# A two-layer graph attention kernel: 22 chunks of rows straight from x, tiles turned two ahead, row buffers in a pool of their own

## The chip, the cores and the metric

The kernel runs on one core of a Trainium2 chip. Its time is the device time of one execution in microseconds (us), from the start of the program to its end, with all loads from and stores to device memory. Three runs of the kernel before gave 4555.35, 4556.34 and 4557.77 us.

## The reference

The graph has N = 6250 nodes with D = 256 features and E = 200000 edges, sorted by destination, with 32 attributes each. Cut to what matters:

```python
h = relu(layernorm(x))                               # rows are normalised over their 256 features
for l, H in ((0, 4), (1, 1)):                        # two layers of graph attention, 4 heads and 1
    te = relu(ea @ We + be) * exp(h @ Wo + bo)[src]  # features of the edges, gated by the source node
    s, d, e = edges and one self loop for each node  # a loop's e is the mean of the edges into its node
    hx = h @ Wg
    al = leaky_relu((hx @ a_s)[s] + (hx @ a_d)[d] + (e @ Wge) @ a_e, 0.2)
    al = softmax of al over the edges with one destination
    out = segment_sum(hx[s] * al, d) + bg + h        # relu of this after layer 0
    h = out
return x + (out + relu(layernorm(x)))
```

So each layer first needs a table with a row for each node (hx, two products with the attention vectors, and the gate), and then fetches 200000 rows of this table, one for each edge.

## The kernel before, in words

**Chunks, steps and tables.** Edges lie in order of destination, 128 to a chunk, one on each partition: 1563 chunks (NCH). 24 chunks make a step (C); a layer has 66 steps (NS), the last two shorter (14 and 13 chunks). The table of layer 0, T[0], has rows of 270 floats: hx, the attention products, the gate, and the two layer norm numbers of the node. Each step handles a window of at most 112 destination nodes.

**The prologue (L203 to L401)** makes T[0] and does all that is needed before the first step. The 6250 rows of x are 49 tiles of 128 rows (NT). They are loaded in groups: two tiles, then five, then seven each, of which the last seven are split into five and two. Four things happen to a tile.

- Its layer norm numbers come from `stats` of its group (L258): for each tile a bn_stats and a bn_aggr, on DVE (VectorE), then a reciprocal square root by three Newton steps (L273 to L298). For groups 0 to 2 these run on DVE; from group 3 on, POOL (GpSimd) does them, 15 instructions; for groups of rows that come straight from x (below) it is DVE again.
- `norm` (L309, ACT, which is ScalarE) makes h; `turn` transposes it with two matmuls into PSUM (L315, PE) and copies it to SBUF (L317, ACT); `mult` multiplies it with the weights (L430, PE); `keep` adds the bias and writes the table row to SBUF (L434, DVE).
- `store` (L332 to L334) finishes the rows of a group, two small ACT instructions, and sends one DMA on SP's queue to T[0].
- The loop at L356 sets the order by hand. In one pass k of it, tile k+3 is normalised, tile k+1 turned, tile k multiplied, and tile k−1 kept. Between these, `step` issues one instruction of the statistics of a later group, at most two groups ahead, and twice as often from the x rows on.

Step 0 does not use the table. Its 24 chunks (CX) are rows of x, fetched by source index with 24 indirect DMAs on POOL (`first_rows`, L247): eight before the loop, one in each pass from k = 4. They are tiles 49 to 72, in four groups of six, and go through the same pipeline into the buffer G0 of step 0. Nothing of them has to be stored. In between stands the index work (`indices` L436, one of its instructions in every second pass; `index_group` L561): numbers that say where segments begin and end, as penalties, flags and offsets. `indices` also writes a small table `flags` (L498) by DMA on SP. Penalties are written once for each of four heads, the copies on ACT (L602).

**The steps (L615 on).** For each step k the loop issues the gathers of the next step and the computation of this one. `gather` (L792) fetches 24 rows per partition from the table with 24 indirect DMAs on POOL (L799), each followed by a memset of a buffer that nobody reads (L803). Three buffers of gathered rows are used in turn, so the gathers of step k+3 go to the buffer of step k. `nodes` (L860) loads the rows of the destination window into one of five tiles (`tws`, cleared at L631). `spread` (L914), `rphase1`, `rphase2`, `adst` and `edge_rows` work out the part of the logits that comes from the edges; `logits` scans them with the penalties for maxima within segments; `scale` multiplies the gathered rows by their weights (L1095, DVE); `sums` adds up by destination with 24 matmuls (L1105); `evict` copies the sums out of PSUM (L1110, ACT), and from then on the buffer of the gathered rows is free. `finish` and `rows1` to `rows3` make the rows of the next layer's table, or of the output.

**What sets the order.** All code of prologue and steps stands under a manual schedule: each engine runs its instructions in the order in which the program issues them, and waits by semaphores for the buffers that it needs. Pools hand out SBUF; a buffer in a pool that opens later can lie where one of a closed pool was, and its first writer then waits for the last readers there. The gather buffers 1 and 2, `S` and the work tiles of the steps come after the prologue's pools.

Memory for gathered rows is `[128, 24, 270]` floats for each of three buffers. At the end `rows3` writes the output; its last rows go by an indirect DMA on POOL (L1249), and `flag` (L789) sums what `indices` found about the indices.

Of the kernel before, what the change touches and what calls it, by code (L numbers as in the profile page):

```python
# [22 lines left out]
F32 = mybir.dt.float32  # L23
# [11 lines left out]
NX = 24  # L35
# [44 lines left out]
class Kernel:  # L80
# [122 lines left out]
    def prologue(self):  # L203
# [7 lines left out]
        with ExitStack() as c:  # L211
            xp = self.pool("x", 1, c)
            wp = self.pool("pw", 2, c)
            pt = self.pool("pt", 2, c, space=PSUM)
            starts = sorted({*range(0, NT, GT), min(2, NT), max(NT - 2, 0)} - {NT})
# [11 lines left out]
            src0 = wp.tile([P, CX], I32, name="src0", bufs=1)  # L227
# [5 lines left out]
            warm = pt.tile([P, 2, P], F32, name="pT")  # L233
            for i in range(28):
                nc.tensor.matmul(warm[:, i % 2, :], self.ident, self.ident, start=True, stop=True)
            self.index_tiles()
            self.fixed_rows()
            zero = wp.tile([P, 2 * L.TW], F32, name="zero", bufs=1)
# [3 lines left out]
            trows = [wp.tile([P, GT, L.TW], F32, name=f"trow{i}", bufs=1) for i in range(3)]  # L242
# [12 lines left out]
            for _ in range(8):  # L255
                next(rows0, None)

# [43 lines left out]
            for i in range(0, CX, 6):  # L301
                xs[len(groups)] = G0[:, i:min(i + 6, CX), 0:D]
                groups.append(list(range(NT + i, NT + min(i + 6, CX))))
# [7 lines left out]
            def turn(g, i, t):  # L311
                pT = pt.tile([P, 2, P], F32, name="pT")
# [3 lines left out]
                hTs[t] = wp.tile([P, 2, P], F32, name="hT", bufs=3)  # L316
# [21 lines left out]
            for _ in range(6):  # L338
                next(lead, None)
            weave(lead, first)  # L340
            ahead = {g: stats(g) for g in range(1, len(groups))}

            def step(g):

                for q in list(ahead):
                    if q > g:
                        return
# [8 lines left out]
            for k in range(-3, len(tiles) + 1):  # L356
# [10 lines left out]
                if 0 <= k + 1 < len(tiles):  # L367
                    turn(*tiles[k + 1])
                if 0 <= k + 3 < len(tiles):
                    g, i, t = tiles[k + 3]  # L370
# [5 lines left out]
                if t >= NT:  # L376
                    step(g + 2)
# [3 lines left out]
                if t >= NT:  # L381
                    step(g + 2)
                if k >= 4:
                    next(rows0, None)
# [18 lines left out]
    def fixed_rows(self):  # L403
# [19 lines left out]
        for i in range(2):  # L423
            self.trow1.append(cp.tile([P, 2 * L1.TW], F32, name=f"t1row{i}"))
            nc.gpsimd.memset(self.trow1[i][:, L1.TW + D:], 0.0)

# [9 lines left out]
    def indices(self, wp):  # L436
# [4 lines left out]
        V = nc.vector  # L441
# [13 lines left out]
        V.tensor_copy(scf, sc0)  # L455
        V.memset(scf[:, 0, 0:1], 0.0)
        self.base_f = base = cp.tile([P, NS], F32, name="base")
        V.tensor_copy(base, scf[:, 0, :])
# [4 lines left out]
        V.tensor_sub(qd, base.unsqueeze(1).to_broadcast([P, 4, NS]), qbase)  # L463
# [1003 lines left out]
```

## Time and profile before

| quantity | value |
|---|---|
| median of three runs | 4556.34 us |
| profiled execution | 4555.93 us |
| its span in the profile | 4554.1 us |
| instructions | 37613 |
| PE, matmuls | 3065.9 us busy (67%), 9916 instructions |
| DVE | 2901.8 us (64%), 6675 |
| ACT | 516.8 us (11%), 1150 |
| POOL | 3915.8 us (86%), 6365 |
| granted TensorE clock, mean | 0.743 |
| read from device memory | 542.72 MB |

The profile is of one execution. A row of its groups names a line of the kernel, the engine, the operation and what it writes and reads, then how often, the busy time and the mean duration in ns; behind the second bar stands how long the engine was idle just before, and what released it. A row of the timeline gives the start of an instruction from the start of the span in us, how long it took, and in square brackets how long the engine had waited before it and for which instruction. "SPq" are the DMAs that SyncE issued, and an instruction that is released by "issue" waited for nothing that the trace shows. A row of the waits gives engine, line and releaser, then the time waited in all, how often, and the longest.

The slices of the span, each a fortieth of it or 114 us, tell the two parts apart: in the first one POOL is busy six tenths and ACT five; in all others up to the last POOL is at eight and ACT at one or none.

```profile
ACT  5111111111111111111100000000000000000000
POOL 6888888888888888888878888888888888888885
```

### The profile page before, as it was taken

Reading aid. Unit: us, or ns where it says so; the run is one execution under the profiler, and the core shown is the slowest. Engines: PE = TensorE matmul, PEld = TensorE weight load, DVE = VectorE, ACT = ScalarE, POOL = GpSimd, SP = SyncE. Lnnn points to the kernel's source line nnn. Section 1 sums busy time; section 2 is a strip of 40 time slices with the busy share of each in tenths; the row PEclk is TensorE's granted clock in tenths of the full one; section 3 lists DMA queues with packets and bytes.
Section 4 is the critical chain, followed back from the end, with each engine's and each line's share of the span. In section 5 each row is a group of like instructions: output and inputs, shape, how many; then the busy total and the mean of one; then the engine's idle time right before and its main releaser. Section 6 shows DMA issues by size and latency. Waiting matters only on the chain. (4 is left out here: it accounts for less than half of the span.)

```text
span 4554.1 us, 37613 instructions
## 1 busy us (share of the span) xinstructions
PE 3065.9 (67%) x9916; PEld 1899.5 (42%) x9916; DVE 2901.8 (64%) x6675; ACT 516.8 (11%) x1150; POOL 3915.8 (86%) x6365
## 2 busy tenths in 40 slices
PE   8777677667677677677746566666666665666665
PEld 6444444444444344444424334333343343433433
DVE  7877667677677677676745555555554555555655
ACT  5111111111111111111100000000000000000000
POOL 6888888888888888888878888888888888888885
PEclk9877777777777777777767777777777777777777
DMA  6444444444444444444434444444444444444442
GB/s 224 130 136 134 126 129 136 124 127 136 125 128 135 125 128 135 125 130 134 119 98 124 116 128 122 118 128 128 111 128 121 124 123 128 122 116 122 128 116 74
DMA packets 231112, 576.39 MB, mean 127 GB/s; under 512 B 63097, under 2 KB 87871, under 8 KB 230825
## 3 DMA queue, kind: packets, MB, share of 16 engines
q0 software_dynamic: 150144, 422.75, 35.2%
q1 hardware_dynamic: 80331, 150.52, 10.0%
q8 instruction: 79, 1.29, 0.1%
q14 instruction: 142, 1.16, 0.1%
q10 hardware_dynamic: 416, 0.67, 0.1%
HBM read 542.72 MB, written 31.09 MB: 126 GB/s over the span
## 5 line engine op out<-in xcount | busy, mean ns | idle before, releaser
L799 POOL DMA_INDIRECT G<-T,src x3102 | 2969.6, 957 | 553.1 <-issue 518.7
L1105 PE MATMUL u<-G,S 128*128 128x270 f32 (+1 forms) x6252 | 1461.0, 393 | 106.7 <-DVE G L1085 97.6
L1105 PEld LDWEIGHTS u<-G,S 128*128 128x128 f32 x6252 | 1189.5, 192 | 388.0 <-DVE G L1085 162.1
L803 POOL MEMSET gap<- 128x208 f32 x3102 | 893.3, 288 | 1.8
L1095 DVE TENSOR_TENSOR G<-G,kps 128x6144 f32<-128x6144 f32 (+3 forms) x136 | 853.0, 6274 | 0.0
L885 PE MATMUL y<-ea,webd 64*128 64x384 f32 (+1 forms) x1056 | 749.7, 860 | 67.3 <-ACT R L890 66.7
L1010 PE MATMUL lf<-ident,fb 128*36 128x128 f32 (+1 forms) x132 | 53.3, 404 | 1093.3 <-DVE fb L1002 772.3
L987 DVE TENSOR_TENSOR G<-rt,G 128x96 f32<-128x96 f32 (+1 forms) x132 | 30.2, 228 | 1138.9 <-DMA G<-T,src 1138.6
L1010 PEld LDWEIGHTS lf<-ident,fb 128*36 128x36 f32 (+1 forms) x132 | 15.7, 119 | 1134.6 <-DVE fb L1002 819.2
L899 PE MATMUL zad<-R,wea 128*64 128x384 f32 (+1 forms) x1056 | 476.0, 815 | 0.5 <-DVE aq L952 0.3
L890 ACT ACTIVATE R<-y,webd 128x768 f32<-128x768 f32 x260 | 233.2, 897 | 2015.2 <-PE lf L1027 1647.7
L930 DVE TENSOR_TENSOR S<-kps,loc 128x3072 f32<-128x3072 f32 x132 | 437.5, 3315 | 4.5
L885 PEld LDWEIGHTS y<-ea,webd 64*128 64x128 f32 x1056 | 300.9, 314 | 311.8 <-issue 192.5
L899 PEld LDWEIGHTS zad<-R,wea 128*64 128x64 f32 x1056 | 160.7, 207 | 319.0 <-issue 214.0
L945 PE MATMUL zad<-a,Q 128*128 128x12 bf16 (+1 forms) x132 | 24.9, 188 | 174.6 <-DVE a L943 174.6
L430 PE MATMUL fin<-wg,h1T 128*128 128x260 f32 x264 | 135.3, 667 | 2.3 <-ACT h1T L1200 2.3
L973 DVE STREAM_TRANSPOSE rt<-zad 128x768 f32<-128x768 f32 (+1 forms) x130 | 124.9, 960 | 12.1 <-PE zad L959 11.2
L914 DVE TENSOR_TENSOR lb<-lb,kps 128x1536 bf16<-128x1536 bf16 (+1 forms) x68 | 112.7, 1658 | 0.0
L1110 ACT ACTIVATE U<-u 128x270 f32<-128x270 f32 (+1 forms) x132 | 51.9, 393 | 493.7 <-PE u L1105 493.7
L1041 DVE SCALAR_TENSOR_TENSOR m<-fpen,lf,m 128x24 f32<-128x24 bf16 (+1 forms) x66 | 16.4, 249 | 132.8 <-PE lf L1027 132.6
L945 PEld LDWEIGHTS <-Q 128*128 128x128 bf16 x132 | 13.7, 104 | 208.3 <-DVE a L943 198.6
L430 PEld LDWEIGHTS fin<-wg,h1T 128*128 128x128 f32 x264 | 75.6, 316 | 52.1 <-issue 36.6
(201 smaller groups left out, 2287.5 us busy)
## 6 DMA issues: line engine op xcount, KB each, us to landing
G<-T,src POOLq DMA_INDIRECT x3102, 2.8
ea<-in_ea_dram SPq DMA_DIRECT2D x64, 768.0 KB
lb<-locrow SPq DMA_DIRECT2D x64, 384.0 KB
T<-t1row SPq DMA_DIRECT2D x66, 227.5 KB
tw<-T SPq DMA_DIRECT2D x66, 225.8 KB
tw<-T SPq DMA_DIRECT2D x66, 117.2 KB
tw<-in_x_dram SPq DMA_DIRECT2D x66, 112.0 KB
out_dram<-fb SPq DMA_DIRECT2D x64, 112.0 KB
```

The source lines that it names most:

```text
L430: self.nc.tensor.matmul(ps[:, :L.MW], hT[:, k, :], self.wg[L.l][:, k, :], start=(k == 0), stop=(k == 1))
L799: nc.gpsimd.indirect_dma_start(out=G[:, c, 0:L.TW], out_offset=None, in_=self.rows[L.l][0:n * (1 + L.l), :], in_offset=bass.IndirectOffset ...
L803: nc.gpsimd.memset(self.gap, 0.0)
L885: nc.tensor.matmul(y[:, o], self.webd[l][r, :], ea[r, w], start=True, stop=True)
L890: nc.scalar.activation(R[:, i, :32 * c].rearrange("p (b n) -> p b n", b=2), y.rearrange("p (b n) -> p b n", b=2)[:, :, :16 * c], AF.Relu, ...
L899: nc.tensor.matmul(st["zad"][i * PH:(i + 1) * PH, o], self.wea[l][0], R[:, i, w], start=True, stop=False)
L914: V.tensor_tensor(lb[:, :, :n], lb[:, :, :n], self.k_part.unsqueeze(2).to_broadcast([P, i, n]), op=OP.is_equal)
L930: nc.vector.tensor_tensor(st["S"][:, c0:c1, :], self.k_iota.unsqueeze(1).to_broadcast(w), self.loc[:, o + c0:o + c1].unsqueeze(2).to_broad ...
L973: V.transpose(rv[:, :32 * c].rearrange("p (b n) -> p b n", b=2), z.rearrange("p (b n) -> p b n", b=2)[:, :, :16 * c])
L1010: self.nc.tensor.transpose(self.lf[0:e.shape[1], 1:P + 1], e, self.ident)
L1095: nc.vector.tensor_tensor(v, v, pw[:, c0:c1, :].unsqueeze(3) .to_broadcast([P, c1 - c0, H, L.F]), op=OP.mult)
L1105: nc.tensor.matmul(st["u"][:, :L.W], S[:, i, :], G[:, i, 0:L.W], start=(j == 0), stop=(j == c - 1))
```

## The change

- **Rows of x.** NX goes from 24 to 22: chunks 22 and 23 of step 0 are fetched from the table by `gather`, as those of all other steps are, but with no memset between them. Tiles are 71 and not 73. Six x gathers come before the loop and not eight, and one in every second pass from k = 11 and not one in each from k = 4.
- **Pools.** `src0`, `zero` and the three buffers of table rows (`trow`) move from the prologue's pool pw to a new pool, rows, of one buffer each, that is opened before pw.
- **Order of the tiles.** The loop runs from −4; tile k+4 is normalised, tile k+2 turned. The PSUM tiles of the transposes are two tiles with two places each and not two buffers, `hT` has four buffers and not three.
- **Groups.** A further group starts at tile 4 (groups of 2, 2, 3, 7 … tiles). The x rows are in groups of 2, 4, 6, 6 and 4. `stats` of x rows are not issued before pass k = 49, and the doubled issue of statistics starts at k = 24 and no longer with the x rows. Ahead of the loop, the statistics of group 0 and the fold of the weights are issued one after the other and not woven.
- **Engines.** Five index operations (scf, base, qd, qsel and the last of fl) go from DVE to POOL. The node tiles `tws` are four and not five, lie in the pool of constants, and are cleared by POOL in the prologue and not by DVE at the start of the steps.
- **Penalties.** `pen` holds one value for an edge and not four. For layer 0, each step copies it for the four heads to one of two small tiles, with one ACT instruction at the head of `rphase1`; `logits` reads that.

The line numbers of the kernel after are higher by 4 in `keep` (L438), `mult` (L434), `turn` (L319, L321) and `norm` (L313), and by 8 in `evict` (L1118).

```diff
@@ -32,7 +32,7 @@
 SE = P * C
-NX = 24
+NX = 22
 D = 256
@@ -210,9 +210,10 @@
             xp = self.pool("x", 1, c)
+            rp = self.pool("rows", 1, c)
             wp = self.pool("pw", 2, c)
             pt = self.pool("pt", 2, c, space=PSUM)
-            starts = sorted({*range(0, NT, GT), min(2, NT), max(NT - 2, 0)} - {NT})
+            starts = sorted({*range(0, NT, GT), min(2, NT), min(4, NT), max(NT - 2, 0)} - {NT})
             groups = [list(range(g, e)) for g, e in zip(starts, starts[1:] + [NT]) if g < e]
@@ -224,22 +225,22 @@
             load(0)
-            src0 = wp.tile([P, CX], I32, name="src0", bufs=1)
+            src0 = rp.tile([P, CX], I32, name="src0")
             nc.sync.dma_start(src0, a["src"][:, 0:CX])
...
-            warm = pt.tile([P, 2, P], F32, name="pT")
+            pts = [pt.tile([P, 2, 2, P], F32, name=f"pT{i}", bufs=1) for i in range(2)]
             for i in range(28):
-                nc.tensor.matmul(warm[:, i % 2, :], self.ident, self.ident, start=True, stop=True)
+                nc.tensor.matmul(pts[1][:, 1, i % 2, :], self.ident, self.ident, start=True, stop=True)
             self.index_tiles()
             self.fixed_rows()
-            zero = wp.tile([P, 2 * L.TW], F32, name="zero", bufs=1)
+            zero = rp.tile([P, 2 * L.TW], F32, name="zero")
             nc.gpsimd.memset(zero, 0.0)
...
                 nc.sync.dma_start(self.T[0][NT * P:N + P, :], zero[:N + P - NT * P, :L.TW])
-            trows = [wp.tile([P, GT, L.TW], F32, name=f"trow{i}", bufs=1) for i in range(3)]
+            trows = [rp.tile([P, GT, L.TW], F32, name=f"trow{i}") for i in range(3)]
             ln = wp.tile([P, NT + CX, 2], F32, name="ln", bufs=1)
@@ -252,8 +253,10 @@
             rows0 = first_rows()
-            for _ in range(8):
+            for _ in range(6):
                 next(rows0, None)
+            for t in self.tws:
+                nc.gpsimd.memset(t, 0.0)
@@ -298,9 +301,10 @@
-            for i in range(0, CX, 6):
-                xs[len(groups)] = G0[:, i:min(i + 6, CX), 0:D]
-                groups.append(list(range(NT + i, NT + min(i + 6, CX))))
+            xc = sorted({0, min(2, CX), *range(6, CX, 6), CX})
+            for i, e in zip(xc, xc[1:]):
+                xs[len(groups)] = G0[:, i:e, 0:D]
+                groups.append(list(range(NT + i, NT + e)))
             tiles = [(g, i, t) for g, ts in enumerate(groups) for i, t in enumerate(ts)]
@@ -309,11 +313,11 @@
             def turn(g, i, t):
-                pT = pt.tile([P, 2, P], F32, name="pT")
+                pT = pts[t // 2 % 2][:, t % 2]
                 h = hs.pop(t)
...
                     nc.tensor.transpose(pT[:, k, :], h[:, k * P:(k + 1) * P], self.ident)
-                hTs[t] = wp.tile([P, 2, P], F32, name="hT", bufs=3)
+                hTs[t] = wp.tile([P, 2, P], F32, name="hT", bufs=4)
                 nc.scalar.activation(hTs[t], pT, AF.Copy)
@@ -335,15 +339,14 @@
             lead = stats(0)
-            for _ in range(6):
-                next(lead, None)
-            weave(lead, first)
+            drain(lead)
+            drain(first)
             ahead = {g: stats(g) for g in range(1, len(groups))}
...
                 for q in list(ahead):
-                    if q > g:
+                    if q > (g if k >= NT else min(g, g0)):
                         return
@@ -353,7 +356,7 @@
             tail = iter(range(max(0, N - 2 * P), N + P, P))
-            for k in range(-3, len(tiles) + 1):
+            for k in range(-4, len(tiles) + 1):
                 if k == 6:
@@ -364,23 +367,23 @@
                     nc.sync.dma_start(self.T[1][n0:n0 + w, :], zero[:w, :2 * self.L[1].TW])
-                if 0 <= k + 1 < len(tiles):
-                    turn(*tiles[k + 1])
-                if 0 <= k + 3 < len(tiles):
-                    g, i, t = tiles[k + 3]
+                if 0 <= k + 2 < len(tiles):
+                    turn(*tiles[k + 2])
+                if 0 <= k + 4 < len(tiles):
+                    g, i, t = tiles[k + 4]
                     if i == 0:
...
                 step(g + 2)
-                if t >= NT:
+                if k >= NT // 2:
                     step(g + 2)
...
                 step(g + 2)
-                if t >= NT:
+                if k >= NT // 2:
                     step(g + 2)
-                if k >= 4:
+                if k > 9 and k % 2:
                     next(rows0, None)
@@ -423,6 +426,7 @@
             nc.gpsimd.memset(self.trow1[i][:, L1.TW + D:], 0.0)
+        self.tws = [cp.tile([P, self.L[0].TW + D], F32, name=f"tw{i}") for i in range(4)]
@@ -438,7 +442,7 @@
         NS, NCH, N = self.NS, self.NCH, self.N
-        V = nc.vector
+        V, Z = nc.vector, nc.gpsimd
         sc0 = wp.tile([P, 11, NS], I32, name="sc0", bufs=1)
@@ -452,18 +456,18 @@
         scf = wp.tile([P, 11, NS], F32, name="scf", bufs=1)
-        V.tensor_copy(scf, sc0)
-        V.memset(scf[:, 0, 0:1], 0.0)
+        Z.tensor_copy(scf, sc0)
+        Z.memset(scf[:, 0, 0:1], 0.0)
         self.base_f = base = cp.tile([P, NS], F32, name="base")
-        V.tensor_copy(base, scf[:, 0, :])
+        Z.tensor_copy(base, scf[:, 0, :])
         last, qbase, qlast = scf[:, 1, :], scf[:, 3:7, :], scf[:, 7:11, :]
...
         qd = wp.tile([P, 4, NS], F32, name="qd", bufs=1)
-        V.tensor_sub(qd, base.unsqueeze(1).to_broadcast([P, 4, NS]), qbase)
+        Z.tensor_sub(qd, base.unsqueeze(1).to_broadcast([P, 4, NS]), qbase)
         yield
         self.qsel = cp.tile([P, NS, 4], F32, name="qsel")
-        V.tensor_scalar(self.qsel.rearrange("p s k -> p k s"), qd, self.iota_m, None, op0=OP.add)
+        Z.tensor_scalar(self.qsel.rearrange("p s k -> p k s"), qd, self.iota_m, None, op0=OP.add)
         yield
@@ -492,7 +496,7 @@
         yield
-        V.tensor_scalar(fl, fl, 1.0, BIG, op0=OP.subtract, op1=OP.mult)
+        Z.tensor_scalar(fl, fl, 1.0, BIG, op0=OP.subtract, op1=OP.mult)
         self.flags = self.dp.tile([2, NS, P + 1], F32, name="flags")
@@ -545,7 +549,11 @@
                                                     for n in ("loc", "fpen", "lpen", "isl"))
-        self.pen = cp.tile([P, 4 * NCH + 1], BF, name="pen")
+        self.pen = cp.tile([P, NCH + 1], BF, name="pen")
+        self.nc.gpsimd.memset(self.pen[:, NCH:], -BIG)
+        self.pen4 = [cp.tile([P, 4 * C + 1], BF, name=f"pen4{i}") for i in range(2)]
+        for t in self.pen4:
+            self.nc.gpsimd.memset(t[:, 4 * C:], -BIG)
         self.bad = cp.tile([P, 1 + len(self.groups)], F32, name="bad")
@@ -589,18 +597,13 @@
             yield
-        pv = self.pen[:, 4 * o:4 * (o + w)].rearrange("p (s h c) -> p s h c", h=4, c=c)
         t = pool.tile([P, 4 * C], F32, name="gt", bufs=2)
...
         yield
-        V.tensor_scalar(pv[:, :, 0, :], t3, 1.0, -BIG, op0=OP.min, op1=OP.mult)
-        V.memset(self.pen[:, 4 * (o + w):4 * (o + w) + 1], -BIG)
-        yield
-        for h in range(1, 4):
-            nc.scalar.activation(pv[:, :, h, :], pv[:, :, 0, :], AF.Copy)
-            yield
+        V.tensor_scalar(self.pen[:, o:o + w], t[:, :w], 1.0, -BIG, op0=OP.min, op1=OP.mult)
+        yield
         t = pool.tile([P, 4 * C], F32, name="gt", bufs=2)
@@ -626,9 +629,6 @@
         self.state = {0: None, 1: None}
-        self.tws = [self.np_.tile([P, self.L[0].TW + D], F32, name=f"tw{i}", bufs=1) for i in range(5)]
-        for t in self.tws:
-            nc.vector.memset(t, 0.0)
         self.nodes(steps[0])
@@ -795,7 +795,7 @@
         last = st["C"] - 1
-        for c in (range(0) if st["k"] == 0 and self.CX > last else (last, *range(last))):
+        for c in (range(self.CX, last + 1) if st["k"] == 0 else (last, *range(last))):
             nc.gpsimd.indirect_dma_start(
@@ -860,7 +860,7 @@
         r = self.row(0, s)
-        tw = self.tws[st["k"] % 5]
+        tw = self.tws[st["k"] % 4]
         st["tw"], st["xw"] = tw[:, :L.TW], tw[:, L.TW:L.TW + D]
@@ -877,7 +877,14 @@
         st["R"] = R = self.wp.tile([P, 2, 32 * C], F32, name="R", bufs=1)
-        c = st["C"]
+        c, o, H = st["C"], st["o"], L.H
+        st["pen"] = self.pen[:, o:o + c + 1]
+        if H > 1:
+            st["pen"] = pen = self.pen4[st["k"] % 2]
+            nc.scalar.activation(pen[:, :H * c].rearrange("p (h c) -> p h c", c=c),
+                                 self.pen[:, o:o + c].unsqueeze(1).to_broadcast([P, H, c]), AF.Copy)
+            if c < C:
+                nc.vector.memset(pen[:, H * c:H * c + 1], -BIG)
         for i in range(2):
@@ -992,14 +999,15 @@
         yield
-        n, p0 = H * c, 4 * o
+        n = H * c
+        pen = st["pen"]
         fb, w = self.fb[st["k"] % 2], c if H > 1 else 1
...
         st["ends"] = fb[:, c - 1:c + (31 + H) * w:w]
-        V.tensor_tensor_scan(f, self.pen[:, p0:p0 + n], al[:, :n], -BIG, op0=OP.add, op1=OP.max)
-        yield
-        V.tensor_tensor_scan(b[:, ::-1], self.pen[:, p0 + 1:p0 + n + 1][:, ::-1], al[:, :n][:, ::-1], -BIG,
+        V.tensor_tensor_scan(f, pen[:, :n], al[:, :n], -BIG, op0=OP.add, op1=OP.max)
+        yield
+        V.tensor_tensor_scan(b[:, ::-1], pen[:, 1:n + 1][:, ::-1], al[:, :n][:, ::-1], -BIG,
                              op0=OP.add, op1=OP.max)
```

## The prediction

> **What bounds the kernel now.** The page comes first: one engine is busy nearly throughout, and two of its lines make up most of that.
>
> ```profile
> span 4554.1 us, 37613 instructions
> ...
> L799 POOL DMA_INDIRECT G<-T,src x3102 | 2969.6, 957 | 553.1 <-issue 518.7
> ...
> L803 POOL MEMSET gap<- 128x208 f32 x3102 | 893.3, 288 | 1.8
> ```
>
> POOL issues 3102 gathers, each followed by a spacing memset, and is idle 0.17 us before each by nothing but issue. A gather that starts to the next that starts is some 1.40 us, and 3102 of these are 4357 us of the 4554. So the question is never what an engine costs beside this stream, only when the stream starts and where it stands still. The waits of POOL tell the second.
>
> ```profile
> POOL G L799 <- issue: 518.7, 3096, 2.0
> POOL out_dram L1249 <- DVE flagf L789: 26.6, 1, 26.6
> POOL fa L1178 <- DVE mw L1155: 21.0, 2, 11.4
> POOL G L799 <- ACT h L309: 17.9, 1, 17.9
> POOL G L799 <- DMA T<-t1row: 10.2, 1, 10.2
> ...
> POOL G L799 <- ACT U L1110: 5.8, 1, 5.8
> ```
>
> Only three of 3102 gathers wait for other work. 17.9 is the wait for the prologue, 10.2 (with 21.0) lies between the layers, 26.6 is the end: the chain of waits starts there and is too short to help. The 5.8 decides this case. The timeline of POOL shows both early waits in place.
>
> ```profile
> 89.29 1.25 POOL L799 DMA_INDIRECT G<-T,src  x1 [17.90 <-ACT h L309]
> ...
> 156.51 0.30 POOL L803 MEMSET gap<- 128x208 f32 x1
> 162.62 0.95 POOL L799 DMA_INDIRECT G<-T,src  x1 [5.81 <-ACT U L1110]
> ```
>
> The stream starts at 89.29 with step 1, and steps 1 and 2 are issued by 156.81. Step 3 needs the buffer of step 0 (three buffers in turn). That is free only when step 0 is summed and evicted, so POOL stands still until 162.62. From there everything to the end follows at a fixed distance. The time after is therefore 4554.1 + (R − 162.62), where R is the start of step 3's gathers: the later of *stream* (last table store landed, plus the gathers before step 3) and *buffer* (step 0 evicted). Later steps have room: the eviction of step 26 ends 38.6 us before the gather that takes its buffer.
>
> ```profile
> 1005.23 0.40 ACT L1110 ACTIVATE U<-u 128x270 f32<-128x270 f32 x1 [1.59 <-PE u L1105]
> ```
> ```profile
> 1044.19 0.95 POOL L799 DMA_INDIRECT G<-T,src  x1 [0.17 <-issue]
> ```
>
> **The change part by part.** *Steady state.* The three broadcast copies of the penalties per group become one ACT copy per step of layer 0, at the head of rphase1, where ACT waits for the matmul anyway. Four tw tiles for five make SP wait for the finish of two steps before; what is queued behind it on SP (the next lb, ea, row stores) is used about a step later, and 38.6 us of room cover that. I cost both at 0; without that cover the copy would cost 0.27 us in each of 65 steps.
>
> *Two chunks fewer from x.* Step 0 gets two gathers through the table, after its last store and ahead of step 1. Without a memset between them they are spaced like the x gathers, 1.25 us: + 2.5 on stream. In return tiles are 71 and not 73.
>
> *When the last store lands (S).* I follow the tiles by hand. In undisturbed stretches a tile takes 1.12 us, and PE has no idle noted in them; turning two ahead can't shorten that, only bridge a late tile.
>
> ```profile
> 111.05 0.38 PE L315 MATMUL pT<-ident,h 128*128 128x128 f32 x2
> ...
> 112.17 0.38 PE L315 MATMUL pT<-ident,h 128*128 128x128 f32 x2
> ```
>
> The start is statistics on DVE.
>
> ```profile
> 5.57 0.17 DVE L273 TENSOR_SCALAR sc<-mv 128x2 f32<-128x2 f32 x1
> ...
> 12.65 0.17 DVE L273 TENSOR_SCALAR sc<-mv 128x5 f32<-128x5 f32 x1
> ...
> 15.07 0.16 DVE L295 SCALAR_TENSOR_TENSOR ln<-mv,sc 128x5 f32<-128x5 f32 x1
> ...
> 23.36 0.60 ACT L309 ACTIVATE h<-x,ln 128x256 f32<-128x256 f32 x1 [0.23 <-DVE ln L295]
> ```
> ```profile
> L176 DVE TENSOR_TENSOR wtmp<-wg,row 128x256 f32<-128x256 f32 x8 | 3.3, 417 | 0.6 <-DMA row<-in_row_dram 0.6
> ```
>
> A chain from L273 to L295 takes 15.23 − 12.65 = 2.6. Group 0 is done at 5.6 + 2.6 = 8.2; the eight fold operations, no longer woven in, take 8 × 0.4 = 3.2, to 11.4. Group 1 (now two tiles) takes 1.0 + 2.6, to 15.0; group 2 (three tiles) 1.3 + 2.6, to 18.9. Group 3 (tiles 7 to 13) has its Newton steps on POOL, as groups from index 3 have, and so tile 7 is now served by POOL and not by DVE. Seven statistics with two results between them and the aggregates take 4.3, to 23.2. On POOL:
>
> ```profile
> 28.16 0.21 POOL L281 TENSOR_TENSOR sc<-sc 128x7 f32<-128x7 f32 x1 [6.05 <-DVE sc L275]
> ...
> 32.52 0.26 POOL L298 TENSOR_SCALAR ln<-sc 128x7 f32<-128x7 f32 x1
> ...
> 34.36 0.94 POOL L249 DMA_INDIRECT G<-in_x_dram,src  x1 [0.31 <-issue]
> 35.60 0.95 POOL L249 DMA_INDIRECT G<-in_x_dram,src  x1 [0.30 <-issue]
> ```
> ```profile
> 32.82 0.60 ACT L309 ACTIVATE h<-x,ln 128x256 f32<-128x256 f32 x1 [1.85 <-POOL ln L298]
> ...
> 45.02 0.60 ACT L309 ACTIVATE h<-x,ln 128x256 f32<-128x256 f32 x1 [4.93 <-POOL ln L298]
> ...
> 56.14 0.60 ACT L309 ACTIVATE h<-x,ln 128x256 f32<-128x256 f32 x1 [2.24 <-POOL ln L298]
> ```
>
> 15 instructions are 4.6. Tile 7 is normalised at 23.2 + 4.6 + 0.1 = 27.9 (23.36 before: 4.5 later). The next group's chain starts when tile 6 is kept (31.8, two keeps behind tile 7's transposes): tile 14 at 36.5 against 32.82. Here the sparser x gathers pay back: POOL had six (7.4 us) ahead of the next chain and now has two, but also the index operations taken from DVE. POOL's price for these is not in the trace. I bound it by
>
> ```profile
> L1186 POOL TENSOR_SCALAR fb<-fb 128x256 f32<-128x256 f32 x2 | 1.7, 855 | 0.2
> ...
> L1180 POOL TENSOR_TENSOR fa<-fa,hw 128x256 f32<-128x256 f32 x2 | 1.4, 722 | 0.0
> ```
> ```profile
> L455 DVE CAST scf<-sc 128x726 f32<-128x726 int32 x1 | 0.5, 540 | 0.0
> ```
>
> The cast of 726 elements lies between DVE's 0.54 and POOL's tensor_scalar stretched by size, 2.4; I take 1.7 with the copy behind it. The subtraction of 264 is 0.74 and qsel 0.87 by the nearest rows. So tile 21's chain starts at 36.4 + 1.7 + 1.25 + 0.74 + 1.25 = 41.4 and ends at 46.0 (45.02 before); tile 28's at 46.0 + 0.87 + 3 × 1.25 = 50.7, and the tile is normalised at 55.4 against 56.14. The loss of the start is made up by tile 28, no more. From there both run at 1.12, tile 48 after 20 tiles.
>
> Before, the last store hung on this row, 3.3 us ahead of 89.29:
>
> ```profile
> 85.98 0.21 ACT L333 ACTIVATE trow<-trow 128x2 f32<-128x2 f32 x1 [0.71 <-DVE trow L434]
> ```
> ```profile
> 63.81 0.73 SPq L498 DMA_DIRECT2D flags<-fl  x2
> ```
>
> Now the statistics of tiles 51 to 54 are held back and then drained at once: four statistics and a chain, 4.4 us of DVE ahead of the results of tiles 46 to 48. That row comes at about 86.6, S is then 86.6 + 3.3 = 89.9. The flags' last operation is now behind nine chains in POOL's queue: they are written near 76 and not 63.81, and hold two 938 KB stores behind them on SP; for the bunching I add 0.5 (between 0 and 2). **S = 90.4**, and stream = 90.4 + 2.5 + (156.81 + 0.17 − 89.29) = **160.6**.
>
> *When step 0 is evicted.* In the old order:
>
> ```profile
> 87.16 0.16 DVE L295 SCALAR_TENSOR_TENSOR ln<-mv,sc 128x6 f32<-128x6 f32 x1
> ...
> 95.94 0.23 DVE L295 SCALAR_TENSOR_TENSOR ln<-mv,sc 128x6 f32<-128x6 f32 x1
> ```
> ```profile
> 116.70 0.43 DVE L434 TENSOR_TENSOR G<-ps,bias 128x266 f32<-128x266 f32 x1 [0.46 <-PE ps L430]
> ...
> 117.68 2.71 DVE L631 MEMSET tw<- 128x524 f32 x5 [0.35 <-issue]
> 118.90 0.37 SPq L866 DMA_DIRECT2D tw<-T  x1
> ...
> 120.30 1.69 DVE L914 TENSOR_TENSOR lb<-lb,kps 128x1536 bf16<-128x1536 bf16 x1
> ```
>
> 162.62 is 45.9 after the last result is kept (116.70). The 2.7 of memsets go to POOL's early idle time and the tw load moves ahead with them: 43.2 remain; next to be late is L914, on DVE itself. The last result: the second group of x rows has its statistics at 90.7 (after the drain), the third 8.8 later as between the two rows above (the list between is nearly the same), the fourth 7.5 later with four tiles, at 107.0, then six tiles at 1.12 from its first transposes: 114.5. Buffer = 114.5 + 43.2 = **157.7**.
>
> *The sum.* R is the later one, 160.6: 2.0 us earlier than 162.62. The profiled execution took 4555.93 (span 4554.1 and 1.8 around it), so 4553.9; the median of the three runs, 4556.34, is 0.4 above it. I predict **4554.3**, a change that a measurement of this kernel can hardly tell (0.2%, or 9 us, is about what it tells from none).
>
> By the Trainium skill (SBUF — State Buffer, Who interferes with whom), a DVE instruction with two SBUF inputs and a POOL instruction that reads SBUF take one shared port in turn, for whole instructions. That speaks against work moved to POOL; here the Newton chain on POOL stayed near 4.6 with DVE busy beside it, and every chain stretched by one 0.4 us keep would put stream at 162.
>
> **Rivals.**
> 1. *Held-back statistics starve PE, and buffer decides: slower.* The DVE queue between tile 51 and tile 70 is nearly full. I used start-to-start distances (a keep 0.34); at mean durations (a keep 0.43, as its busy time has it) three groups take 1.9 more each, and the last result is kept at 120.2. It decides from 117.4 and is slower than before from 119.4: R = 163.4, + 0.8, and with the start 3 us later too + 4. For: before, ACT waited for DVE's statistics here as well. Against: distances are measured.
> 2. *Fewer x gathers and two-ahead turning remove the stalls* at tiles 14, 21 and 28 (1.85 + 4.93 + 2.24 by ACT's rows). If the start cost only 3 of these 9: S = 85, stream 155.2, buffer about 153: R = 155.2, − 7.4. Against: tile 7 now waits for POOL, and two-ahead asks for a late tile one matmul earlier.
> 3. *The pools do not separate as meant*: step 1's gathers wait for a reader in the new place until the prologue ends (116). R = 116 + 2.5 + 67.7 = 186: + 24. Against: they cover x's buffers, whose last reader is tile 48.
> 4. *Contention.* Gathers average 957 ns; the fastest take 951, so POOL loses 6 ns × 3102 = 19 us to something in the stream. If the change doubled or halved that, + 19 or − 9. Against: the DVE work beside the stream is the same, and keeps its place by waiting for each gather.
>
> **How the numbers follow.** Forecast, R from 158 to 163: 0.68 (4551 to 4556.5). Rival 1: 0.16. Rival 2: 0.09. Rival 3: 0.03. Rival 4: 0.04. Rivals 1 and 2 stay mostly within 9 us. The range takes in the bounds of the POOL prices (1.5), of the bunching (1.5) and most of rivals 1 and 2: 4548 to 4561. Faster by over 0.2%: 0.05; within: 0.89; slower: 0.06.
>
> **What would show it.** First table gather of step 0 at 89 to 92; ACT's waits for POOL's statistics at tiles 7, 14, 21 and 28, the first near 27.9; a pause of DVE's results near tile 47; the last result near 114.5; no wait, or one under 2 us, of step 3's gathers for U; steps 3 on at the same distances, and 3104 gathers. A wait for U of over 2 us means that buffer decides (rival 1); steps 1 or 2 that wait long mean rival 3; a gather mean other than 957 ns means rival 4.

## The result and the profile after

The kernel after takes 4565.5 us (median of 13 runs, 4562.8 to 4567.81), the kernel before 4555.35 us in 13 runs beside it. The ratio is 1.0022, with a 95% interval of 1.0014 to 1.0029: 6 to 13 us slower. Forecast were 4554.3 us and a difference too small to measure. The profiled execution took 4565.69 us, 9.8 more than that of before, and its span is 9.7 longer.

The page of after: its first line and the group of the gathers. The stream is what it was, 3104 gathers and 958 ns for 957.

```profile
span 4563.8 us, 37645 instructions
...
L799 POOL DMA_INDIRECT G<-T,src x3104 | 2972.6, 958 | 546.2 <-issue 518.1
```

The waits of POOL show a new one. The wait for U (5.8 us before) is gone. This one stands where before had its 17.9 us for ACT, ahead of the first gather from the table, and it names the store of the table rows.

```profile
POOL G L799 <- DMA T<-trow: 16.1, 1, 16.1
```

The timeline of POOL, at the last gather of x rows, the first two of the table, and step 3:

```profile
83.43 0.95 POOL L250 DMA_INDIRECT G<-in_x_dram,src  x1 [0.30 <-issue]
100.47 0.94 POOL L799 DMA_INDIRECT G<-T,src  x1 [16.09 <-DMA T<-trow]
...
102.96 0.95 POOL L799 DMA_INDIRECT G<-T,src  x1 [0.30 <-ACT h L313]
```
```profile
170.32 0.95 POOL L799 DMA_INDIRECT G<-T,src  x1 [0.17 <-issue]
```

POOL is done with the x rows at 84.4 and waits 16.1 us for the table in memory. The stream starts at 100.47, not at 89.29; step 1 follows 2.5 later, and step 3 starts at 170.32 without a wait. That is 7.7 after the 162.62 of before. What follows step 3 takes 4563.8 − 170.32 = 4393.5, before 4554.1 − 162.62 = 4391.5: 2.0 more. Together the 9.7.

The timeline of ACT in after: the last row of the table, and the eviction of step 0.

```profile
89.21 0.19 ACT L337 ACTIVATE trow<-trow 128x2 f32<-128x2 f32 x1
```
```profile
161.00 0.40 ACT L1118 ACTIVATE U<-u 128x270 f32<-128x270 f32 x1 [15.11 <-PE u L1113]
```

The row is ready at 89.40. Before, it was 86.19 and the stream started 3.1 later; now the gap is **11.1 us**. The buffer of step 0 would have let step 3 start at 161.40 + 0.34 = 161.7.

What the DMAs do in that gap is seen on SP's timeline, before and then after (lb, ea and fl are the loads for step 0), and in stretches of 5 us, from 75 to 90 before and from 75 to 100 after. Their last two columns are the DMA engines' busy share and GB/s.

```profile
70.84 1.30 SPq L826 DMA_DIRECT2D ea<-in_ea_dram  x1
...
77.56 8.98 SPq L334 DMA_DIRECT2D T<-trow  x3
```
```profile
78.06 0.71 SPq L502 DMA_DIRECT2D flags<-fl  x2
78.86 0.36 SPq L338 DMA_DIRECT2D T<-trow  x1
...
79.97 1.29 SPq L826 DMA_DIRECT2D ea<-in_ea_dram  x1
...
82.55 7.20 SPq L338 DMA_DIRECT2D T<-trow  x3
```
```profile
75.00:80.00 5.00, 5.00 (x29) 4.18 (x28) 4.65 (x31) 3.30 (x10) 0.00 (x0) 1.00 0.91 262
80.00:85.00 5.00, 3.30 (x16) 2.18 (x15) 4.72 (x25) 3.02 (x9) 0.00 (x0) 1.00 0.40 164
85.00:90.00 5.00, 4.97 (x28) 3.98 (x27) 4.86 (x24) 3.74 (x11) 0.71 (x1) 1.00 0.39 154
```
```profile
75.00:80.00 5.00, 5.00 (x28) 4.15 (x27) 4.68 (x23) 3.91 (x10) 3.94 (x10) 1.00 0.11 38
80.00:85.00 5.00, 4.87 (x26) 3.73 (x24) 4.43 (x20) 2.79 (x8) 3.46 (x4) 1.00 0.95 250
85.00:90.00 5.00, 2.30 (x9) 1.91 (x10) 4.76 (x21) 2.73 (x10) 0.00 (x0) 0.85 1.03 271
90.00:95.00 5.00, 4.32 (x18) 3.12 (x18) 4.55 (x28) 2.62 (x7) 0.00 (x0) 0.81 0.89 346
95.00:100.00 5.00, 4.45 (x24) 3.40 (x22) 4.80 (x30) 2.81 (x7) 0.00 (x0) 1.00 0.15 62
```

SP reaches the flags at 63.81 before and at 78.06 after, and everything behind them moves: ea from 70.84 to 79.97. Before, the engines are at 0.91 from 75 to 80 and at 0.4 when the last two stores go out. After, they idle from 75 to 80 (0.11) and are full from 80 to 95. From 95 on they are at 0.15, and the last store still lands only near 100; why its end is so slow, the views do not show.

### The profile page after: what moved, and what is told of

Same layout as the page of the kernel before. It is cut to its first block, busy times and chain, and to the rows that moved or that the text cites. A ratio compares the mean times of both kernels' runs of the same rounds, so it can differ in the third digit from the quotient of the medians.

```text
span 4563.8 us, 37645 instructions
## 1 busy us (share of the span) xinstructions
PE 3060.9 (67%) x9904; PEld 1898.1 (42%) x9904; DVE 2898.8 (64%) x6659; ACT 518.5 (11%) x1161; POOL 3927.1 (86%) x6393
## 5 line engine op out<-in xcount | busy, mean ns | idle before, releaser
L434 PE MATMUL fin<-wg,h1T 128*128 128x260 f32 x264 | 134.8, 664 | 2.3 <-ACT h1T L1208 2.3
L1118 ACT ACTIVATE U<-u 128x270 f32<-128x270 f32 (+1 forms) x132 | 51.9, 393 | 491.2 <-PE u L1113 491.2
L434 PEld LDWEIGHTS fin<-wg,h1T 128*128 128x128 f32 x264 | 75.4, 315 | 52.1 <-issue 36.6
```

Source lines behind the costliest of these rows:

```text
L434: self.nc.tensor.matmul(ps[:, :L.MW], hT[:, k, :], self.wg[L.l][:, k, :], start=(k == 0), stop=(k == 1))
```

## The experiments

Theories: **1**, the loads for step 0, let go late by the flags, share the DMA engines with the last table stores; **2**, the spread x gathers do; **3**, only the held-back statistics count. "Gap" is the time from the end of the instruction that finishes the last row to the start of the first table gather, in the one execution that was profiled: 3.1 us before, 11.1 after.

The first four ran on a chip on which the kernel before takes 4738 us and on which the kernel after was not run. There step 3 waits 29 us or more for step 0's buffer (last section), so of these only the prologue up to the first table gather is read.

**a_fl**

```diff
-        Z.tensor_scalar(fl, fl, 1.0, BIG, op0=OP.subtract, op1=OP.mult)
+        V.tensor_scalar(fl, fl, 1.0, BIG, op0=OP.subtract, op1=OP.mult)
```


> The kernel after, with the last operation of the flags (L499) back on DVE; all else as after. In the profile of after the first table gather starts at 100.5 us, 11 us after the last table row is ready (89.4), and step 3's gathers start at 170.3; the buffer of step 0 would have let them start at 161.7. Theory 1 (SP stands behind the flags until 78.06, so a table store and the loads of lb and ea for step 0 run into the last three stores): flags written before 70, the last store lands 3 to 4.5 us after its row is ready, first gather 92.5 to 94, time 4557.5 to 4559. Theory 2 (the x gathers that are spread out to 83 us fill the DMA engines): they stay where they are, first gather 97 to 100, time 4562 to 4565. Theory 3 (only the held-back statistics count): no change, 4565.5.

Measured: 4754.31 us, 1.003 (1.0014 to 1.0046) of before there. Last row 89.0, first gather 94.43, gap 5.4: a little over the 3 to 4.5 of theory 1, and half of after's.

**a_xg**

```diff
-            for _ in range(6):
+            for _ in range(8):
...
-                if k > 9 and k % 2:
+                if k >= 4:
                     next(rows0, None)
```


> The kernel after, with its 22 x gathers issued as in the kernel before (eight ahead of the loop, one in each pass from k = 4); the flags' last operation stays on POOL, behind the chains. Theory 1: POOL has three gathers fewer ahead of that operation, so flags are written near 74 and not 78; the first table gather is 4 us earlier at most, 96 to 97, time 4561 to 4562. Theory 2: nothing else is on the DMA engines then, first gather 92.5 to 94, time 4557.5 to 4559. Theory 3: no change, 4565.5.

Measured: 4758.02 us, 1.0043 (1.0026 to 1.006). First gather 98.68, which no theory forecast, behind a last row at 95.4: the gap is 3.3, but the rows come 6 us later than in a_fl. So the run does not decide between 1 and 2: SP issues ea at 81.05, no earlier than in after, but the last two stores only at 93.37 and 95.39. ACT waits for POOL's statistics, of tile 21 and of tile 28:

```profile
53.41 0.60 ACT L313 ACTIVATE h<-x,ln 128x256 f32<-128x256 f32 x1 [6.14 <-POOL ln L301]
64.35 0.60 ACT L313 ACTIVATE h<-x,ln 128x256 f32<-128x256 f32 x1 [0.80 <-POOL ln L301]
```

In a_fl these stand at 47.99 and 57.99. The x gathers ahead of the chains on POOL cost some 6 us; spreading them is a gain of the change, not its loss.

**a_both** (the two edits together)

> The kernel after, with both edits: the flags' last operation on DVE and the x gathers as before. Theories 1 and 2 both give a first gather at 92.5 to 93 and a time near 4557.5 (the buffer of step 0 becomes the bound at 161.7); theory 1 says that this is the time of the flags' edit alone, theory 2 that it is the time of the x gathers' edit alone. If both count in part, each alone gives a part and this one the whole. Theory 3: 4565.5.

Measured: 4760.9 us, 1.0038 (1.0023 to 1.0054). Last row 94.5, first gather 97.87: the rows are as late as in a_xg. No theory had this.

**a_late** (the three loads issued when the last group is stored)

```diff
                     next(index)
-                    self.load_lb(0)
-                    self.load_ea(0)
-                    self.load_fl(0)
...
                     kept += 1
+                    if kept == g0:
+                        self.load_lb(0)
+                        self.load_ea(0)
+                        self.load_fl(0)
```


> The kernel after, with the three loads for step 0 (lb, ea, fl) issued on SP behind the last table store instead of ahead of the last three; the flags are still written at 78. It divides theory 1: if the 1.15 MB of lb and ea in front of the stores are what delays them, the first table gather starts at 93 to 95 and the time is 4558 to 4560, or longer by what step 0 then waits for ea (it is read at 124 in the profile of after). If the late flags alone delay the stores, by holding them back on SP, it stays at 99 to 100.5 and near 4565.

Measured: 4746.56 us, 1.0026 (1.001 to 1.0042). Flags still at 77.5; last row 87.1, first gather 91.70, gap 4.6. So either edit alone, a_fl's or a_late's, leaves a gap of about half of after's 11.1.

The next four, on a chip like that of the first runs (before 4556.23):

**c1** is a_fl and a_late together.

> The kernel after, with the flags' last operation back on DVE and the loads of lb, ea and fl for step 0 issued behind the last table store. Theory 1 (the loads of step 0 stand on the DMA engines in front of the last stores): the first table gather comes 3.3 to 4.6 us after the last table row is ready, and not 11.1; with rows ready at 89.4 it starts at 92.7 to 94, step 3's gathers at 162.6 to 163.9 and not at 170.3, time 6.5 to 7.7 us less than after on a chip like that of the first runs (4558 to 4559 against 4565.5). Rival (the rows themselves or the statistics set it): gap of 11 as before, no change of the time. On a chip where the granted clock falls behind 115 us, only the start up to there is compared.

Measured: 4556.29 us, 1.0 (0.9991 to 1.0009). POOL:

```profile
89.21 0.95 POOL L800 DMA_INDIRECT G<-T,src  x1 [7.74 <-DMA T<-trow]
```
```profile
159.20 0.95 POOL L800 DMA_INDIRECT G<-T,src  x1 [0.17 <-issue]
```

Last row 85.8, gap 3.4: the loss is gone. Step 3 starts 11.1 us earlier than in after and not 6.5 to 7.7, since the last row came 3.6 earlier too, which was not expected (c2 shows how much of that is scatter). The profiled execution took 4564.05 in spite of its early step 3. It is the longest of the eleven, and its gathers average 961 ns, not 958: 3 ns by 3104 are 9 us. Single executions scatter by so much, so the starts are read from traces and the times from medians.

**c2** is c1 with statistics not held back.

```diff
-                    if q > (g if k >= NT else min(g, g0)):
+                    if q > g:
```


> c1, and the statistics of x rows are no longer held back until k = 49. Held back, they are drained ahead of the results of tiles 46 to 48, and the last table row is ready at 89.4 against 86.2 before. If that is the cause of these 3.2 us: last row at 86 to 87, first gather at 89.5 to 91, last result of step 0 kept at 115 to 117 and not 118.9, step 3's gathers near 159.5 to 161, time 4554 to 4556. If the late start of the pipeline (tile 7 by POOL) is the cause, the last row stays near 89 and the time is that of c1.

Measured: 4557.47 us, 1.0002 (0.9993 to 1.0011). The last row is ready at 91.6, not earlier but 5.8 later than in c1. Most of that is not the edit, which acts on the statistics of tiles 51 on (those of tiles 49 and 50 are not held back): up to the norm of tile 47, c1 and c2 run the same instructions in the same order, and it stands 5.3 us apart. ACT, in c1 and then in c2:

```profile
75.28 0.59 ACT L313 ACTIVATE h<-x,ln 128x256 f32<-128x256 f32 x1
```
```profile
80.60 0.59 ACT L313 ACTIVATE h<-x,ln 128x256 f32<-128x256 f32 x1
```

So much can two executions of one order of instructions differ. Counted from these rows, the last row is ready after 10.5 us in c1 and 11.0 in c2, and the last result of step 0 is kept after 40.8 and 39.4. Holding the statistics back delays the last row by nothing and the last result by 1.3 us. Theory 3 falls.

**b_ealate** is the kernel before with only the loads moved.

```diff
                     next(index)
-                    self.load_lb(0)
-                    self.load_ea(0)
-                    self.load_fl(0)
...
+                if k == 46:
+                    self.load_lb(0)
+                    self.load_ea(0)
+                    self.load_fl(0)
                 while kept < g0 and groups[kept][-1] <= k - (3 if k < NT - 3 else 1):
```


> The kernel before, with one thing moved: the loads of lb, ea and fl for step 0 are issued in pass 46, behind the store of tiles 35 to 41, and not in pass 43. SP then issues them at about 78 and not at 70. Theory 1: they share the DMA engines with the last two stores, the first table gather starts at 93 to 97 and not at 89.3 with the last row still ready at 86.2; step 3 was held by the buffer at 162.6, with 5.6 us of room for the stream, so the time is longer by 0 to 2 us only. Rival (the late flags or the x gathers are needed for it): the first gather stays at 89.3 to 90.

Measured: 4556.23 us, 1.0 (0.9991 to 1.0009). SP, ACT and POOL:

```profile
76.76 1.29 SPq L827 DMA_DIRECT2D ea<-in_ea_dram  x1
```
```profile
84.08 0.21 ACT L333 ACTIVATE trow<-trow 128x2 f32<-128x2 f32 x1 [0.72 <-DVE trow L435]
```
```profile
92.57 1.08 POOL L800 DMA_INDIRECT G<-T,src  x1 [23.24 <-DMA T<-trow]
```

The gap grows from 3.1 to 8.3 with nothing else changed, though the row itself comes 1.9 earlier than before's: theory 1 in its purest form. Theory 2 falls with it as the whole cause, since the last x gather here ends at 49.2. The 3 to 5 us that after and after2 (below) have on top of 8.3 are not divided between the x gathers and the store that the flags held back. As expected the time hides it, since step 3 waits for U anyway (1.9 us, until 161.80).

**b_tws** is the kernel before with the four node tiles (cleared by POOL) and the short penalties of the change, as its diff shows them (NX stays 24); the short penalties make the room.

```diff
+        self.tws = [cp.tile([P, self.L[0].TW + D], F32, name=f"tw{i}") for i in range(4)]
...
+            for t in self.tws:
+                nc.gpsimd.memset(t, 0.0)
...
-        self.tws = [self.np_.tile([P, self.L[0].TW + D], F32, name=f"tw{i}", bufs=1) for i in range(5)]
-        for t in self.tws:
-            nc.vector.memset(t, 0.0)
```


> The kernel before, with the node tiles and the penalties of the change alone: four tiles cleared by POOL in the prologue, one penalty for an edge and an ACT copy in each step of layer 0. All else as before (24 chunks of x rows, tiles one ahead). By the terms of the prediction: the 2.7 us of memsets on DVE go, so step 0 is evicted at 159.6 and not 162.3, step 3's gathers start at 159.9, the first table gather stays at 89.3; 2.7 us less, 4553.6 against 4556.3. If the copy or the four tiles cost something in the steps, step 131 starts later against step 3 than the 4332.3 us of before, by up to 18 us (0.27 in each of 65 steps).

Measured: **4551.39 us**, 0.999 (0.9981 to 0.9999) of before: 0.5 to 8.7 us faster, better than both kernels. ACT and POOL:

```profile
157.60 0.40 ACT L1117 ACTIVATE U<-u 128x270 f32<-128x270 f32 x1 [15.02 <-PE u L1112]
```
```profile
158.33 0.95 POOL L798 DMA_INDIRECT G<-T,src  x1 [2.33 <-ACT pen L883]
```

Step 3 starts 4.3 earlier than before (2.7 were expected), when the eviction ends at 158.00 (the row names the ACT copy that follows it). What follows takes 4550.1 − 158.33 = 4391.8, as before (4391.5): the copy and the four tiles cost nothing in the steps.

The last four, on one more chip (before 4559.17):

**after2** is the kernel after, unchanged.

> The kernel after once more, unchanged, for the scatter of its own prologue beside the two edits of this batch. In its first profile the last table row was ready at 89.4 and the first table gather started at 100.5. Expected: 86 to 90 and 97 to 101 (a gap of 10 to 11.5), time 4564 to 4567. If the gap comes out under 6, theory 1 explains the first profile only and not the median.

Measured: 4570.55 us, 1.0025 (1.0016 to 1.0035), over the expected range on a chip that is slower for before too, by 3.8 us. Last row 89.3, first gather 102.14, gap 12.9. It is no accident of one execution.

**a_fl2** is a_fl again.

> The kernel after with the flags' last operation back on DVE, and the loads for step 0 in their old place ahead of the last three stores. Theory 1: SP leaves the flags near 66, the loads are issued near 73 and are through before the last two stores; gap of 3.1 to 5.5 between last row and first gather, first gather 91 to 94.5, time 4556 to 4560. Rival (the place of the loads alone, not the time at which SP issues them): gap 9 to 11, time 4564 to 4567.

Measured: 4563.91 us, 1.0009 (1.0 to 1.0018), over the expected range, by about what the chip is slower. SP and POOL, last row 89.2:

```profile
73.92 1.50 SPq L826 DMA_DIRECT2D ea<-in_ea_dram  x1
```
```profile
94.35 0.94 POOL L799 DMA_INDIRECT G<-T,src  x1 [9.40 <-issue]
```

Gap 5.1. The row names no releaser; that POOL waits here for the stores is read from its place, at the first gather from the table. Against after2 it is 6.6 us less by the medians, 8.0 by the starts of step 3 (164.35 and 172.37).

**a_late2** is a_late again.

> The kernel after with the loads for step 0 behind the last table store, and the flags still late (last operation on POOL). Theory 1: nothing but stores and x gathers is then on the DMA engines, gap of 3.3 to 5, first gather 91 to 94, time 4556 to 4560. Rival (SP held by the flags counts by itself): gap 8 to 11, time 4562 to 4567.

Measured: 4563.82 us, 1.001 (1.0001 to 1.0019), again over the expected range. SP and POOL, last row 90.0:

```profile
80.15 0.71 SPq L503 DMA_DIRECT2D flags<-fl  x2
...
91.01 0.51 SPq L827 DMA_DIRECT2D ea<-in_ea_dram  x1
```
```profile
94.34 0.94 POOL L800 DMA_INDIRECT G<-T,src  x1 [7.88 <-DMA T<-trow]
```

Gap 4.4 with the flags as late as ever, and with x gathers up to 86.5. So SP's standing still does little harm by itself; what it lets go at the wrong time does.

**c3** is c1 with the start of the kernel before.

```diff
-            drain(lead)
-            drain(first)
+            for _ in range(6):
+                next(lead, None)
+            weave(lead, first)
...
-            starts = sorted({*range(0, NT, GT), min(2, NT), min(4, NT), max(NT - 2, 0)} - {NT})
+            starts = sorted({*range(0, NT, GT), min(2, NT), max(NT - 2, 0)} - {NT})
```


> c1 (flags on DVE, loads behind the last store) with the start of the kernel before: no group start at tile 4, statistics of group 0 woven with the fold. By the prediction the loss of 4 us at tile 7 is made up by tile 28, because the chains on POOL pace the tiles: tile 7 is normalised near 23.4 and not 27, but tile 28 near 54 to 55 as in c1 (54.8 for the first wait behind it), last row within 1 us of c1's 85.8, time within 1 us of c1's 4556.3. If the start does count: last row 3 to 4 us earlier, first gather near 86, and the buffer (156.7 in c1) then bounds, 2 to 2.5 us less: 4554.

Measured: 4557.32 us, 0.9996 (0.9987 to 1.0005). ACT at tile 28, and POOL:

```profile
52.62 0.60 ACT L313 ACTIVATE h<-x,ln 128x256 f32<-128x256 f32 x1 [2.21 <-POOL ln L301]
```
```profile
87.06 0.95 POOL L801 DMA_INDIRECT G<-T,src  x1 [7.76 <-issue]
```

Last row 83.5. On the same chip a_fl2 has tile 28 at 58.21 and its last row at 89.2: the start of the change costs up to 5.6 us, and tile 28 does not make it up. Against c1, on the other chip, it is 2.2 at tile 28 (54.77) and 2.3 at the last row. With a scatter like that between c1 and c2 the size is open. Step 3 starts at 157.0, but the time is not clear of before's, nor of b_tws's.

## Why the prediction was wrong

**The structure held.** R, the start of step 3, is the later of stream and buffer, and all behind it moves along: 7.7 of the 9.7 us. The fixed parts were right: two gathers through the table cost 2.5 (102.96 − 100.47), and from step 1 to step 3 it is 67.4 (67.7 forecast).

**The step that failed is S**, the landing of the last store: 90.4 forecast, 100.5 found. Its parts, counted as in the forecast from the start of the instruction that finishes the last row: that row, 86.6 forecast and 89.2 found (2.6), and the landing, where "for the bunching I add 0.5 (between 0 and 2)" stood for what was 8.0 (11.3 instead of 3.3). The flags had been seen: "near 76" forecast, 78.06 found. That they "hold two 938 KB stores behind them on SP" was seen as well. What was left out is that lb and ea, 1.15 MB, stand in the same queue ahead of the last three stores, and that the engines, idle in their old place, are then full. By bytes the price could have been set: stores of 938, 938, 670 and 268 KB, 1.15 MB of loads and five x gathers of 128 KB are 4.6 MB, and at the 250 to 350 GB/s of the rows above 13 to 18 us from 79 on. This estimate gives 92 to 97, not 90, and is still short of 100.5, because the end was slow (62 GB/s from 95 to 100).

By the Trainium skill (DMA: Bandwidth & Descriptors, Queues, rings and completion order) each engine takes a queue's descriptors in the order of issue, and (Issuing engines are not separate DMA queues) DMAs issued by SP and POOL run on the same 16 engines and interleave. The traces agree: with the flags late, the gap is 4.4 with the loads behind the stores (a_late2) and 11 to 13 with them ahead (after, after2).

**The tiles** came out close: ACT's waits for POOL's statistics at tiles 7, 14, 21 and 28 were forecast for 27.9, 36.5, 46.0 and 55.4.

```profile
27.13 0.60 ACT L313 ACTIVATE h<-x,ln 128x256 f32<-128x256 f32 x1 [4.87 <-POOL ln L301]
37.59 0.60 ACT L313 ACTIVATE h<-x,ln 128x256 f32<-128x256 f32 x1 [0.19 <-POOL ln L301]
46.15 0.60 ACT L313 ACTIVATE h<-x,ln 128x256 f32<-128x256 f32 x1 [0.91 <-POOL ln L301]
56.56 0.60 ACT L313 ACTIVATE h<-x,ln 128x256 f32<-128x256 f32 x1 [2.97 <-POOL ln L301]
```

That they come so close is in part luck: in the eight executions with the change's start and its sparse gathers, tile 28 lies between 54.8 and 58.7. The reason given was half right: by a_both and a_fl (last rows at 94.5 and 89.0) the sparser gathers gain 5.5 us, and by c3 the start loses 2 to 6 that tile 28 does not make up. Of the 2.6 us of the last row, 1.2 stand at tile 28. The rest comes right behind it, where PE's granted clock (third number from the end) is low in this execution, and tile 35 follows 8.7 us after tile 28. In after2 the clock is full there, and it is 7.1. After, then after2:

```profile
55.00:60.00 5.00, 2.92 (x11) 2.23 (x11) 4.03 (x18) 2.40 (x7) 4.02 (x11) 0.78 0.98 331
60.00:65.00 5.00, 5.00 (x26) 3.98 (x25) 2.60 (x10) 3.41 (x10) 3.92 (x15) 0.88 0.36 119
```
```profile
55.00:60.00 5.00, 3.33 (x18) 2.48 (x17) 4.68 (x22) 2.40 (x9) 3.83 (x12) 1.00 0.78 274
60.00:65.00 5.00, 5.00 (x29) 4.20 (x29) 3.80 (x20) 4.03 (x12) 3.93 (x16) 1.00 0.75 268
```

**Buffer** was 157.7 in the forecast and is 161.7. Here rival 1 was right in part: the last result is kept at 118.85 and not at 114.5.

```profile
118.85 0.43 DVE L438 TENSOR_TENSOR G<-ps,bias 128x266 f32<-128x266 f32 x1 [0.46 <-PE ps L434]
```

It costs nothing, because stream is later. Of the 4.3 us, 2.6 came with the rows; by c1 and c2 the holding back is worth 1.3, so rival 1's mechanism is there but small. From the last result to the start that step 0's eviction allows (161.7) it is 42.9, 43.2 forecast. In b_tws the same stretch is 42.2 and before 45.9, so the memsets and what goes with them are worth 3.7 us where 2.7 were taken. Rival 3 did not occur; of rival 4 there are 2 us at most.

**Open:** six of the seven kernels with 22 chunks that ran on the other three chips are 1.6 to 3.8 us longer by their medians than their step 3 says (after 10.2 against 7.7; c2 is 0.6 shorter), each inside its interval; of the two with 24 chunks, b_ealate is 0.8 longer and b_tws 0.6 shorter. Whether 22 chunks lose something in the steps is not settled.

## What to carry to other kernels

Where a wait is added on a queue that issues DMAs, list what stands behind it with its bytes, and ask what it will share the DMA engines with when it is let go: here the same 1.15 MB cost little behind the awaited stores (gap 3.4 to 4.6) and 5.2 us beside them (b_ealate, 8.3 against 3.1). Issue what is awaited first and the bulk that is needed later behind it. A bound on such a term comes from bytes over the rate that the profile shows, not from a feeling for bunching. And before a few us of a prologue are put down to an edit, look where the two traces part: if that is ahead of the edit's first effect, it is scatter.

## What the runs showed of the hardware

- The same program runs differently from chip to chip: on one, the kernel before took 4738 us. In a_late there, the granted clock (third number from the end) was 0.68 from 105 to 125 us, and step 3 waited 29.3 us for step 0's buffer. With the same kernel on another chip (a_late2) it was 0.93, and step 3 did not wait. The stretch in a_late, then in a_late2, and the wait in a_late:

```profile
105.00:125.00 20.00, 9.03 (x31) 6.69 (x29) 5.35 (x21) 4.46 (x11) 17.68 (x29) 0.68 0.43 116
```
```profile
105.00:125.00 20.00, 16.11 (x74) 12.42 (x74) 14.71 (x51) 8.82 (x24) 17.61 (x29) 0.93 0.52 130
```
```profile
POOL G L800 <- ACT pen L885: 29.3, 1, 29.3
```

- POOL's prices, which the forecast had to bound: a cast of 726 elements 0.79 us (1.7 taken, with a copy of 0.24), a tensor_scalar of 264 with a strided result 1.45 (0.87 taken).

```profile
37.50 0.79 POOL L459 CAST scf<-sc 128x726 f32<-128x726 int32 x1
...
46.10 1.45 POOL L470 TENSOR_SCALAR qsel<-qd,iota_m 128x264 f32<-128x264 f32 x1
```
